# Weights of an involution made for two tile rows at once: 64 stationary columns instead of 32

## The chip, the cores and the metric

The kernel runs on one core of one Trainium2 chip. The time is the device time of one launch in microseconds (us). The runs are few and scatter by some tenths of a per cent, so medians are compared. Engines: PE is TensorE (its weight loads, PEld, overlap its matmuls), DVE is VectorE, ACT is ScalarE, POOL is GpSimd, SP is SyncE, which here only issues DMAs.

## The reference, cut to what matters

Two layers, each added to its input, on x of shape (32, 256, 32, 32) in float32: 32 images, 256 channels, 32 x 32 pixels.

```python
# layer 0: a 3x3 convolution 256 -> 256 in fp16, after a group norm
x = x + _L0_conv_ref(_gn(x), weight, bias)
# layer 1: an involution, after a group norm
x = x + _L1_conv_ref(_gn(x), w1, bn_gamma, bn_beta, bn_mean, bn_var, w2, b2)

def _L1_conv_ref(x, w1, bn_gamma, bn_beta, bn_mean, bn_var, w2, b2):
    y = einsum('oc,bchw->bohw', w1, x)              # 256 -> 64 features
    y = relu(y * scale + shift)                     # a batch norm with fixed numbers
    w = einsum('oc,bchw->bohw', w2, y) + b2         # 64 -> 16 groups x 49 taps
    # each pixel has its own 7x7 kernel for each of 16 groups of 16 channels
    out = einsum('bgkhw,bgckhw->bgchw', w.reshape(b, 16, 49, H, W), patches(x, 7, pad=3))
```

The change is in how `w` is made, 64 features to 784 numbers at every pixel, and how it is laid out for the last sum.

## The kernel before, in words

**Front.** `front(b)` is a generator that does one image up to the features: group norm on ScalarE, the 3x3 conv in fp16 on TensorE (L337, 72 matmuls of 128x128 with up to 512 columns, accumulated in `pc`), clamp and residual on VectorE (L351, L353), a second group norm into `xn`, the 1x1 conv to 64 features (`py`, L385), and their ReLU by ScalarE into `y_sb` (L392). `y_sb` has the 64 features on 64 partitions twice: rows 0 and 1 of every four image rows in the lower half of the partitions, rows 2 and 3 in the upper one. At last the pixels of `xn` are transposed (`pt`, L400) and copied into `pixels` (L404).

**Weights.** `weights(b, r0)` makes the taps of four image rows in one call, 8 calls an image. For each of two rows in a half and each of four pairs `t` of tap columns dj, the 32 pixels of a row are the stationary operand (64 features x 32 pixels), and two tap columns of `w2_sb` (2 x 112 numbers; the last pair has one, 112) are the moving rows. So 16 matmuls go to 8 tiles of the array, 2 row halves by 4 column quadrants of 32, into two PSUM tiles `pw0` and `pw1`. In the trace each fp32 matmul and its weight load leave two records each. `evict` (L439) adds the bias on VectorE and writes the taps to `w_sb`, ordered by the source row that a tap reaches (image row plus tap row minus 3), in a ring of 32 rows. Where a call's pieces cross the image's edge or the ring's end, `ring_pieces` splits them, into 4 to 8 evictions a call.

**Through DRAM.** `scatter(b, k, part)` (L480, 7 DMAs per k of 160 KB, issued by SP) writes the rows of tile row k (8 image rows, 4 tile rows an image) from `w_sb` to the DRAM tile `wd`, one tap column dj a DMA, shifted so that each source pixel has its window. `load_bands(b, k)` (L493, 14 DMAs on POOL's queue and 2 on SP's) reads them back as a band, with three bands in turn.

**Sums.** `sums(b, m)` (L518) multiplies the pixels (64 positions x 32 channels stationary, again 8 tiles of 64x32) by the band (up to 190 window pixels moving) into `acc`, and `add_windows` (L534, VectorE) adds a window to x. `store` writes x out.

**Order.** `manual_schedule` keeps the order of the program on every engine, and a loop over steps n writes it by hand. An image has 16 steps. In each step come first the fronts of some three images, one stage each, then `sums` (even steps, two per tile row), `add_windows` a step later, `weights` (even steps, 18 steps ahead of the same image's sums), scatters, the load of x, and the band loads (9 steps ahead of their sums, every fourth step). In steps relative to the first sums of an image:

| tile row k | scattered in steps | band loaded in step | its first sums in step |
|---|---|---|---|
| 0 | -13, -12 | -9 | 0 |
| 1 | -9, -8 | -5 | 4 |
| 2 | -5, -4 | -1 | 8 |
| 3 | -3, -2 | 3 | 12 |

Call c of `weights` (0 to 7) stands in step 2c - 18. On TensorE an even step thus runs: part of a front (conv, features or transposes), sums, weights; then an odd step's front, and so on.

Of the kernel before, what the change touches and what calls it, by code (L numbers as in the profile page):

```python
# [9 lines left out]
F32 = mybir.dt.float32  # L10
AF = mybir.ActivationFunctionType
ALU = mybir.AluOpType

P = 128
B, C, H, W = 32, 256, 32, 32
N = H * W
NT = 512
# [3 lines left out]
K1, PAD1 = 7, 3  # L21
TAPS = K1 * K1
CR = 64
G = 16
# [15 lines left out]
TR = RG * XR  # L40
SIDES = 2
JC = W // SIDES
K = H // TR
M = K * SIDES
WIN = XR + K1 - 1
# [6 lines left out]
V = 2  # L52
A = G // V
WB = G * WIN
PAD = V * (TR - XR)
WPIX = K1 * WB + PAD
SW = K1 * G
S = H + 2 * PAD1
T = 4
TW = P // T  # L60
PAIR = 3 * GC
PAIRS = G // 2
ROW = S * WPIX
WR = 4
NBAND = 3
SHARE = 8
NPIX = 6
RING = 32
SCRATCH = 4096
FRONT = -56  # L70
LOAD = -63
LEAD = 18
# [3 lines left out]
def tile_quant_conv_then_involution(  # L76
# [16 lines left out]
    nc = tc.nc  # L93
    PSUM = bass.MemoryType.PSUM

    const = ctx.enter_context(tc.tile_pool(name="const", bufs=1))
# [4 lines left out]
    ps_w = ctx.enter_context(tc.tile_pool(name="ps_w", bufs=1, space=PSUM))  # L101
# [39 lines left out]
    for t in sum(sum(sums_sb, []), []):  # L141
        nc.gpsimd.memset(t, 0.0)

    y_sb = [const.tile([P, N // 2], F32, name=f"y_{i}") for i in range(2)]
    bands = [const.tile([P, SIDES, WINC * WB + PAD], F32, name=f"band_{i}") for i in range(NBAND)]
    for t in bands[CH:]:
        nc.gpsimd.memset(t, 0.0)
# [2 lines left out]
        nc.gpsimd.memset(t, 0.0)  # L150


    w_sb = const.tile([P, 2, RING, A, WIN, V], F32, name="w_sb")
    wd = dram.tile([H, S, WPIX], F32, name="wd")
    acc = [ps_acc.tile([P, RG, NT], F32, name=f"acc_{d}") for d in range(SIDES)]

# [2 lines left out]
    for kh in range(CH):  # L159
        wf = bands[kh].rearrange("p d n -> p (d n)")[:, : K0 * K0 * C].rearrange("p (k c) -> p k c", c=C)  # L160
        nc.sync.dma_start(wf, w0[kh * P : (kh + 1) * P])
        staged.append(wf)
    w2_sb = const.tile([P, K1, SW], F32, name="w2_sb")
    for i in range(2):
        nc.sync.dma_start(w2_sb[i * CR : (i + 1) * CR], w2)
    b2_sb = const.tile([P, 2, 2, SW], F32, name="b2_sb")
    for dj in range(K1):
        t, e = divmod(dj, 2)
        for r in range(2):
            nc.sync.dma_start(b2_sb[t * TW : (t + 1) * TW, e, r], b2[dj].partition_broadcast(TW))  # L170

    bias_sb = const.tile([P, CH], F32, name="bias_sb")
    nc.sync.dma_start(bias_sb, bias0.rearrange("(h p) -> p h", p=P))
# [10 lines left out]
    bn_scale = const.tile([P, 1], F32, name="bn_scale")  # L184
    nc.vector.tensor_mul(bn_scale, bn[:, 0:1], bn_r)
    bn_shift = const.tile([P, 1], F32, name="bn_shift")
# [4 lines left out]
    for col, cols, at, n in (  # L191
# [4 lines left out]
        to = bass.AP(  # L196
            tensor=wd.tensor,
            offset=wd.offset + col * WPIX + at,
            ap=[[ROW, H], [WPIX, cols], [1, n]],
        )  # L200
# [88 lines left out]
    def front(b):  # L289
# [30 lines left out]
        for s in range(4 * len(units) + 2):  # L320
            u, i = divmod(s, 4)
            if u < len(units):
# [6 lines left out]
                for n in range(sum(CONV[:i]), sum(CONV[: i + 1])):  # L329


                    k = n if n < K0 * K0 else CH * K0 * K0 - 1 - n
                    kh, k = n // (K0 * K0), (k + K0 * K0 // 2) % (K0 * K0)
                    di, dj = k // K0 - PAD0, k % K0 - PAD0
                    r0, r1 = max(nt * RT, -di), min((nt + 1) * RT, H - di)
# [9 lines left out]
            u, i = divmod(s - 3, 4)  # L345
            if 0 <= u < len(units) and i < 3:
                nt, mh = units[u]
                cols = slice(nt * NT, (nt + 1) * NT)
                if i == 0:
                    q = work.tile([P, NT], F16, tag="q", name="q", bufs=1)  # L350
# [20 lines left out]
        for h in range(CH):  # L371
            yield
            to = xn[:, h].rearrange("p (k d r j) -> p d k r j", d=SIDES, r=TR, j=JC)
            at = xt[:, h].rearrange("p (k r d j) -> p d k r j", d=SIDES, r=TR, j=JC)
# [3 lines left out]
        py = ps_m.tile([P, NT], F32, tag="m", name="py")  # L378
        for r0 in range(0, H, WR):
            cols = slice(r0 // 2 * W, (r0 + WR) // 2 * W)  # L380
            for kh in range(CH):
                px = xn[:, kh].rearrange("p (k d r j) -> p k r d j", d=SIDES, r=TR, j=JC)[:, r0 // TR]
                for i in range(2):
                    r = r0 % TR + 2 * i
# [4 lines left out]
                        start=kh == 0,  # L389
                        stop=kh == CH - 1,  # L390
                    )
        nc.scalar.activation(y_sb[b % 2], py, AF.Relu, bias=bn_shift, scale=bn_scale)  # L392
        yield from stages(5)

        for m in range(0, M, 2):
# [7 lines left out]
            to = pixels[(b * M + m) // 2 % NPIX].rearrange("p i a (v c) -> p (i a) v c", c=GC)  # L403
            nc.scalar.copy(to[:, :, ::2], pt.rearrange("p i (a v c) -> p (i a) v c", v=2, c=GC))  # L404
            yield

    def weights(b, r0):

        pws = [ps_w.tile([P, 2, 2, SW], F32, tag=f"pw{i}", name=f"pw{i}") for i in range(2)]
        for r in range(2):  # L410
            for t in range(T):
                for i in range(2):
                    half = slice(i * CR, (i + 1) * CR)
                    dj = slice(2 * t, min(2 * t + 2, K1))
                    nc.tensor.matmul(  # L415
                        pws[i][t * TW : (t + 1) * TW, : dj.stop - dj.start, r],
                        y_sb[b % 2][half, (r0 // 2 + r) * W : (r0 // 2 + r + 1) * W],
                        w2_sb[half, dj],
                        start=True,
                        stop=True,  # L420
                    )
        for i in range(2):
            for e in range(2):
                p = P if e == 0 else (K1 // 2) * TW
                for r, rows, d0, d1, at in ring_pieces(b, r0 + 2 * i):
                    evict(pws[i][:p, e, r : r + rows], e, r, rows, d0, d1, at)

    def evict(of, e, r, rows, d0, d1, at):

        p = of.shape[0]  # L430
        to = w_sb[:p, e]
        to = bass.AP(
            tensor=to.tensor,
            offset=to.offset + at * WB + V * (K1 - 1 - d0),
            ap=[to.ap[0], [V * WIN, rows * A], [WB - V, d1 - d0], [1, V]],
        )
        of = of.rearrange("p r (a d v) -> p (r a) d v", a=A, v=V)
        bias = b2_sb[:p, e, r : r + rows].rearrange("p r (a d v) -> p (r a) d v", a=A, v=V)
        nc.vector.tensor_tensor(to, of[:, :, d0:d1], bias[:, :, d0:d1], ALU.add)  # L439

    def ring_pieces(b, r0):

        def place(r, d):
            s = r0 + r + d - PAD1
            return (b * H + s) % RING if 0 <= s < H else None

        def together(d):
            return place(0, d) is not None and place(1, d) == place(0, d) + 1  # L450

        pieces = []
        for rows, ok in (
            ((0, 2), together),
            ((0, 1), lambda d: place(0, d) is not None and not together(d)),
            ((1, 1), lambda d: place(1, d) is not None and not together(d)),
        ):
            d = 0
            while d < K1:
                d0 = d  # L460
                while d < K1 and ok(d) and place(rows[0], d) == place(rows[0], d0) + d - d0:
                    d += 1
                if d > d0:
                    pieces.append((*rows, d0, d, place(rows[0], d0)))
                else:
                    d += 1
        return pieces

    def scatter(b, k, part):

        at = (b * H + k * TR) % RING
        for dj in range(part, K1, 2):
            t, e = divmod(dj, 2)
            to = bass.AP(
                tensor=wd.tensor,
                offset=wd.offset + k * TR * ROW + dj * WPIX + (K1 - 1 - dj) * WB,
                ap=[[WPIX, TW], [ROW, TR], [1, WB]],
            )
            rows = w_sb[t * TW : (t + 1) * TW, e, at : at + TR]
            nc.sync.dma_start(to, rows.rearrange("p s a r v -> p s (a r v)"))  # L480

    def load_bands(b, k):

# [61 lines left out]
    def due(n, lag):  # L545

        b, i = divmod(n - lag, per)
        return (b, i) if 0 <= b < B else (None, None)

    with tc.manual_schedule():  # L550
        fronts = {}
        for n in range(FRONT, B * per + 2):
            b, i = due(n, FRONT)
            if i == 0:
                fronts[b] = front(b)
            later = list(fronts)
            for part in range(2):
                for b in list(later):
                    got = next(fronts[b], fronts)
                    if got is fronts:  # L560
                        fronts.pop(b)
                    if got is not LATER:
                        later.remove(b)
            if n == FRONT + CH:
                quantize_weights()
            b, i = due(n, 0)
            if b is not None and i % 2 == 0:
                sums(b, i // 2)
            b, i = due(n, 1)
            if b is not None and i % 2 == 0:  # L570
                add_windows(b, i // 2)
                if i // 2 == M - 1:
                    store(b, 1)
                    x_tiles.pop(b)

            b, i = due(n, 2)
            if b is not None and i == 2 * (M - 1 - SIDES):
                store(b, 0)
            b, i = due(n, -LEAD)
            if b is not None and i % 2 == 0:  # L580
                weights(b, i // 2 * WR)

            for part in range(2):
                b, i = due(n, -LEAD + 1 + part)
                if b is not None and i % 2 == 0:
                    for k in range(K):
                        if i // 2 == min((k + 1) * TR // WR, H // WR - 1):
                            scatter(b, k, part)
            b, i = due(n, LOAD)
            if i == 0 and b > 0:  # L590
                x_tiles[b] = load_x(b)

            b, i = due(n, 3 - 4 * NBAND)
            if b is not None and i % 4 == 0:
                load_bands(b, i // 4)
# [37 lines left out]
```

## Time and profile before

| | |
|---|---|
| median of three runs | 1375.84 us (1371.69 to 1378.53) |
| the profiled execution's own time | 1370.77 us |
| its span, first to last instruction | 1368.9 us |
| granted TensorE clock, mean | 0.988 |
| DMA | 369.93 MB, mean 270 GB/s; 280240 packets on SP's queue, 86016 on POOL's |
| weights, TensorE (L415) | 8192 records, 290.6 us busy |
| sums, TensorE (L518) | 16384 records, 428.5 us busy |
| conv, TensorE (L337) | 2304 records, 534.5 us busy |
| weights, VectorE (L439) | 1280 instructions, 331.4 us busy |
| band loads, POOL (L493) | 1792 DMAs, 978.0 us busy, 4.9 us from issue to landing |

How to read it: "busy" is the time in which at least one instruction of a group ran, so groups that overlap count the same time twice. A matmul's end is modelled and reaches past the point where its last column went in. "x32" counts instructions, and "64*32" is the tile of the array that an instruction uses (rows by columns). In a table of waits a line gives who waited for whom, then the time in total, how often, and the longest; "issue" is idle time without anything shown that holds the engine. In a table of stretches each engine has its busy time and number of instructions, then the granted clock, the DMA engines' busy share and GB/s. "Single records" are the trace's instructions one by one, with start and duration.

### The profile page before, as it was taken

What the parts mean: (1) busy time and instruction counts of PE and PEld (TensorE: products, weight loads), DVE (VectorE), ACT (ScalarE), POOL (GpSimd) and SP (SyncE); (2) the same over time, 40 slices, a digit from 0 to 9 for tenths busy, and PEclk for the clock granted to TensorE, in tenths of its full rate; (3) what the DMA queues carried; (4) which work ended last, traced back from release to release, by engine and by line L of the source; (5) the groups of instructions that cost most, each with busy time, mean ns of one, the idle gap of its engine ahead of it and who ended that gap; (6) DMA issues with size and microseconds to landing.
All of it is one profiled execution on the core that took longest, in us unless ns stands there. A gap on an engine that the chain in (4) does not pass through costs nothing.

```text
span 1368.9 us, 69378 instructions
## 1 busy us (share of the span) xinstructions
PE 1261.3 (92%) x29440; PEld 805.5 (59%) x29440; DVE 820.2 (60%) x2539; ACT 726.8 (53%) x1699; POOL 1012.1 (74%) x1818
## 2 busy tenths in 40 slices
PE   4799999999999999999999999999999999999664
PEld 2356666656665665666666566556656656666543
DVE  3366566666666666665666666656666666666542
ACT  4866565465655555665555565545555555553300
POOL 9057777778777777877777777777777777778875
PEclk9999999999999999999999999999999999999997
DMA  6089999999999999999999999999999999999995
GB/s 218 6 221 289 278 283 290 296 274 287 277 285 284 279 287 282 291 290 282 289 286 285 276 279 282 280 294 269 282 290 278 286 285 287 289 287 268 275 273 170
DMA packets 366563, 369.93 MB, mean 270 GB/s; under 512 B 78960, under 2 KB 308528, under 8 KB 366000
## 3 DMA queue, kind: packets, MB, share of 16 engines
q1 hardware_dynamic: 280240, 235.90, 58.0%
q0 software_dynamic: 86016, 129.60, 34.1%
q8 instruction: 234, 3.83, 1.2%
q14 instruction: 73, 0.60, 0.1%
HBM read 184.43 MB, written 180.76 MB: 267 GB/s over the span
## 4 chain that ended last, share of the span: by engine, by line
PE 72%; DMA 13%; issue 4%; POOL 3%; ACT 3%; SPq 2%; DVE 2%; POOLq 0%; DVEq 0%; ACTq 0%
PE pc L337 29%; PE acc L518 23%; PE pw L415 13%; DMA band<-wd 7%; PE py L385 4%; DMA wd<-w_sb 4%; PE pt L400 3%; POOL band L493 3%; ACT junk L224 1%; SPq L480 1%; DMA x<-in_x 1%; DMA out<-x 1%; DVE w_sb L439 1%; DMA w_sb<-in_w 1%; SPq L493 0%
## 5 line engine op out<-in xcount | busy, mean ns | idle before, releaser
L493 POOL DMA_DIRECT2D band<-wd x1792 | 978.0, 548 | 343.2 <-DMA band<-wd 209.9
L439 DVE TENSOR_TENSOR w_sb<-pw,b_sb 128x224 f32<-128x224 f32 (+7 forms) x1280 | 331.4, 324 | 434.7 <-PE pw L415 428.7
L337 PE MATMUL pc<-xq,wq 128*128 128x496 f16 (+3 forms) x2304 | 534.5, 378 | 30.6 <-ACT xq L283 24.3
L518 PE MATMUL acc<-band,pixels 64*32 64x190 f32 (+1 forms) x16384 | 428.5, 329 | 50.5 <-DMA band<-wd 28.0
L337 PEld LDWEIGHTS <-wq 128*128 128x128 f16 x2304 | 206.5, 98 | 324.3 <-issue 110.9
L518 PEld LDWEIGHTS acc<-band,pixels 64*32 64x32 f32 x16384 | 300.8, 106 | 141.8 <-issue 89.4
L415 PE MATMUL pw<-w_sb,y 64*32 64x224 f32 (+1 forms) x8192 | 290.6, 330 | 17.7 <-issue 16.8
L534 DVE TENSOR_TENSOR x<-acc,x 128x380 f32<-128x380 f32 (+1 forms) x512 | 262.3, 512 | 32.9 <-PE acc L518 24.0
L415 PEld LDWEIGHTS pw<-w_sb,y 64*32 64x32 f32 x8192 | 186.1, 105 | 48.3 <-issue 33.4
L404 ACT COPY pixels<-pt 128x512 f32<-128x512 f32 x128 | 73.7, 576 | 237.2 <-PE pt L400 237.2
L224 ACT ACTIVATE junk<-x 128x512 f16<-128x512 f32 (+1 forms) x192 | 146.4, 763 | 16.6 <-DVE bn_ve L182 6.0
L224 ACT ACTIVATE junk<-x,mean 128x1024 f16<-128x1024 f32 x128 | 147.1, 1149 | 4.3
L255 ACT ACTIVATE s<-back,eps 128x2 f32<-128x2 f32 x64 | 19.0, 296 | 198.6 <-DVE back L240 198.5
L351 DVE TENSOR_SCALAR q<-pc 128x512 f16<-128x512 f32 x128 | 87.1, 680 | 18.2 <-PE pc L337 18.1
L283 ACT ACTIVATE xn<-x,off,rstd 128x512 f32<-128x512 f32 x128 | 96.2, 800 | 0.0
L353 DVE SCALAR_TENSOR_TENSOR x<-q,bias_sb,x 128x512 f32<-128x512 f16 x128 | 94.6, 739 | 0.3
L400 PEld LDWEIGHTS pt<-ident,xn 128*128 128x128 f32 x512 | 63.3, 141 | 26.6 <-issue 2.7
L400 PE MATMUL pt<-ident,xn 128*128 128x128 f32 x512 | 77.3, 274 | 0.8 <-ACT pixels L404 0.7
L283 ACT ACTIVATE xq<-x,off,rstd 128x1024 f16<-128x1024 f32 x64 | 75.8, 1227 | 1.0 <-PE pc L337 0.9
L385 PEld LDWEIGHTS py<-xn,w_sb 128*64 128x64 f32 x2048 | 62.8, 138 | 16.8 <-issue 6.7
L385 PE MATMUL py<-xn,w_sb 128*64 128x64 f32 x2048 | 67.7, 224 | 2.8 <-ACT xn L283 2.2
L245 ACT ACTIVATE mean<-back 128x2 f32<-128x2 f32 x64 | 12.6, 196 | 101.2 <-DVE back L240 101.2
(40 smaller groups left out, 372.7 us busy)
## 6 DMA issues: line engine op xcount, KB each, us to landing
wd<-w_sb SPq DMA_DIRECT2D x896, 160.0 KB
band<-wd POOLq DMA_DIRECT2D x1792, 70.5 KB, 4.9
x<-in_x SPq DMA_DIRECT2D x64, 512.0 KB
out<-x SPq DMA_DIRECT2D x64, 512.0 KB
band<-wd SPq DMA_DIRECT2D x256, 70.5 KB
band<-in_w SPq DMA_DIRECT2D x2, 1152.0 KB
w_sb<-in_w SPq DMA_DIRECT2D x2, 196.0 KB
wd<-band SPq DMA_DIRECT2D x2, 180.0 KB
```

The source lines that it names most:

```text
L224: nc.scalar.activation(junk[:, n0:n1], src[:, h, n0:n1], func, bias=bias, accum_out=self.sums[:, i : i + 1])
L283: nc.scalar.activation(dst, src, AF.Identity, bias=self.off[:, one], scale=self.rstd[:, one])
L337: nc.tensor.matmul(pc.rearrange("p (r c) -> p r c", c=W)[:, r0 - nt * RT : r1 - nt * RT, c0:c1], wq[:, kh, k, mh * P : (mh + 1) * P], xq[: ...
L351: nc.vector.tensor_scalar(q, pc, F16_MAX, -F16_MAX, ALU.min, ALU.max)
L353: nc.vector.scalar_tensor_tensor(xt[:, mh, cols], q, bias_sb[:, mh : mh + 1], xt[:, mh, cols], ALU.add, ALU.add)
L385: nc.tensor.matmul(py[i * CR : (i + 1) * CR, cols], w1_sb[:, kh, :], px[:, r : r + 2], start=kh == 0, stop=kh == CH - 1,)
L400: nc.tensor.transpose(pt[:, i, h * P : (h + 1) * P], xn[:, h, (m + i) * P : (m + i + 1) * P], ident)
L415: nc.tensor.matmul(pws[i][t * TW : (t + 1) * TW, : dj.stop - dj.start, r], y_sb[b % 2][half, (r0 // 2 + r) * W : (r0 // 2 + r + 1) * W], w ...
L439: nc.vector.tensor_tensor(to, of[:, :, d0:d1], bias[:, :, d0:d1], ALU.add)
L493: queue.dma_start(band[j::JC, :, j * WB : j * WB + WPIX], src)
L518: nc.tensor.matmul(at[t * TW : (t + 1) * TW, h, :, f - top : l - top], px[p, a, v * GC : v * GC + TW], of[:, :, a, f - top : l - top, v], ...
L534: nc.vector.tensor_tensor(x_at, of, x_at, ALU.add)
```

## The change

`weights(b, n)` makes taps for two tile rows at once. Four calls serve tile rows 2a and 2a + 1 (a = 0, 1); an image still has 8 calls, in the same steps. For one row rho counted from the top of a tile row (-3 to 10, since rows above and below reach into it), the 32 pixels of that row in tile row 2a and the 32 pixels of the same row in tile row 2a + 1 together are the 64 stationary columns. `y_sb` is laid out so that these 64 lie side by side, with a row of zeros at either end for rows outside of the image. The moving rows are, for four tap columns dj (`QE`; the eighth is zero), the 1 to 7 tap rows d that land inside of the tile row: 64 numbers for each tap row, 64 to 448. Two column quadrants `t` of 64 take tap columns 0 to 3 and 4 to 6. `UNITS` deals the 14 rows rho out to the four calls, two lists for the two halves of the partitions. A call has 8, 8, 8 or 4 matmuls with 512, 448, 448 or 384 columns per tile of the array.

`w_sb` becomes two blocks of two tile rows (a = 0, 1), each 8 source rows by 4 tap columns, of the same size in all; no taps are left out at the image's edge, and no ring is left. Each row rho has one eviction, 14 per a. A scatter still moves 32 partitions x 8 rows x 160 numbers, now from rows that lie four tap columns apart. The scatters of both tile rows of a block wait for its fourth call. In the steps of the table above they are now: k = 0 in -11, -10; k = 1 in -9, -8; k = 2 in -3, -2; k = 3 in -1, 0. The band loads stay in their steps. At the start, `b2_sb` is loaded with 2 DMAs instead of 14, after a memset; `y_sb` (two) and one column block of `w2_sb` get memsets too.

```diff
+BLK = TR
+QB = H // BLK
 T = 4
 TW = P // T
+QT = 2
+QE = 4
+QW = P // QT
-RING = 32
+UNITS = (((4, -3), (3, 10)), ((0, 8), (7, -1)), ((1, 9), (6, -2)), ((5,), (2,)))
...
-    y_sb = [const.tile([P, N // 2], F32, name=f"y_{i}") for i in range(2)]
+    y_sb = [const.tile([P, N // 2 + 2 * W], F32, name=f"y_{i}") for i in range(2)]
+    for t in y_sb:
+        nc.gpsimd.memset(t, 0.0)
...
-    w_sb = const.tile([P, 2, RING, A, WIN, V], F32, name="w_sb")
+    w_sb = const.tile([P, 2, BLK, QE, WB], F32, name="w_sb")
...
-    w2_sb = const.tile([P, K1, SW], F32, name="w2_sb")
+    w2_sb = const.tile([P, QT * QE, SW], F32, name="w2_sb")
+    nc.gpsimd.memset(w2_sb[:, K1:], 0.0)
...
-    b2_sb = const.tile([P, 2, 2, SW], F32, name="b2_sb")
-    for dj in range(K1):
-        t, e = divmod(dj, 2)
-        for r in range(2):
-            nc.sync.dma_start(b2_sb[t * TW : (t + 1) * TW, e, r], b2[dj].partition_broadcast(TW))
+    b2_sb = const.tile([P, QE, SW], F32, name="b2_sb")
+    nc.gpsimd.memset(b2_sb, 0.0)
+    for t in range(QT):
+        dj = slice(t * QE, min((t + 1) * QE, K1))
+        nc.sync.dma_start(b2_sb[t * QW : (t + 1) * QW, : dj.stop - dj.start], b2[dj].partition_broadcast(QW))
...
-        nc.scalar.activation(y_sb[b % 2], py, AF.Relu, bias=bn_shift, scale=bn_scale)
+        to = y_sb[b % 2][:, W:-W].rearrange("p (r k c) -> p k r c", k=QB, c=W)
+        of = py.rearrange("p (k r c) -> p k r c", k=QB, c=W)
+        nc.scalar.activation(to, of, AF.Relu, bias=bn_shift, scale=bn_scale)
...
-    def weights(b, r0):
...
-    def evict(of, e, r, rows, d0, d1, at):
...
-    def ring_pieces(b, r0):
...
+    def weights(b, n):
+
+        a, n = divmod(n, len(UNITS))
+        pws = [ps_w.tile([P, NT], F32, tag=f"pw{i}", name=f"pw{i}") for i in range(2)]
+        ats = [0, 0]
+        for rhos in zip(*UNITS[n]):
+            for i, rho in enumerate(rhos):
+                d0, d1 = max(0, PAD1 - rho), min(K1, BLK + PAD1 - rho)
+                d = d1 - d0
+                of = pws[i][:, ats[i] : ats[i] + QE * d * G]
+                k, r = divmod(rho, BLK)
+                half = slice(i * CR, (i + 1) * CR)
+                y0 = (((r // 4) * 2 + r % 2) * QB + 2 * a + k) * W + W
+                for t in range(QT):
                     nc.tensor.matmul(
+                        of[t * QW : (t + 1) * QW].rearrange("p (q n) -> p q n", n=d * V),
+                        y_sb[b % 2][half, y0 : y0 + QW],
+                        w2_sb[half, t * QE : (t + 1) * QE].rearrange("p e (a n) -> p (e a) n", a=A)[:, :, V * d0 : V * d1],
                         start=True,
                         stop=True,
                     )
+                ats[i] += QE * d * G
+        ats = [0, 0]
+        for rhos in zip(*UNITS[n]):
+            for i, rho in enumerate(rhos):
...
+                to = bass.AP(
+                    tensor=to.tensor,
+                    offset=to.offset + (rho + d0 - PAD1) * QE * WB + V * (K1 - 1 - d0),
+                    ap=[to.ap[0], [V * WIN, QE * A], [QE * WB - V, d], [1, V]],
+                )
...
+                nc.vector.tensor_tensor(to, of, bias, ALU.add)
+                ats[i] += QE * d * G
...
     def scatter(b, k, part):
 
-        at = (b * H + k * TR) % RING
+        a, k2 = divmod(k, 2)
         for dj in range(part, K1, 2):
-            t, e = divmod(dj, 2)
+            t, e = divmod(dj, QE)
...
-            rows = w_sb[t * TW : (t + 1) * TW, e, at : at + TR]
-            nc.sync.dma_start(to, rows.rearrange("p s a r v -> p s (a r v)"))
+            p = t * QW + k2 * TW
+            nc.sync.dma_start(to, w_sb[p : p + TW, a, :, e])
...
             if b is not None and i % 2 == 0:
-                weights(b, i // 2 * WR)
+                weights(b, i // 2)
 
             for part in range(2):
-                b, i = due(n, -LEAD + 1 + part)
-                if b is not None and i % 2 == 0:
-                    for k in range(K):
-                        if i // 2 == min((k + 1) * TR // WR, H // WR - 1):
-                            scatter(b, k, part)
+                for k in range(K):
+                    b, i = due(n, -LEAD + 1 + part + k % 2 * 2)
+                    if b is not None and i == 8 * (k // 2) + 6:
+                        scatter(b, k, part)
```

More of the change, by code (lines that the diff above doesn't have):

```diff
@@ L162, in tile_quant_conv_then_involution @@
         staged.append(wf)
-    w2_sb = const.tile([P, K1, SW], F32, name="w2_sb")
+    w2_sb = const.tile([P, QT * QE, SW], F32, name="w2_sb")
+    nc.gpsimd.memset(w2_sb[:, K1:], 0.0)
     for i in range(2):
-        nc.sync.dma_start(w2_sb[i * CR : (i + 1) * CR], w2)
-    b2_sb = const.tile([P, 2, 2, SW], F32, name="b2_sb")
-    for dj in range(K1):
-        t, e = divmod(dj, 2)
-        for r in range(2):
-            nc.sync.dma_start(b2_sb[t * TW : (t + 1) * TW, e, r], b2[dj].partition_broadcast(TW))
+        nc.sync.dma_start(w2_sb[i * CR : (i + 1) * CR, :K1], w2)
+    b2_sb = const.tile([P, QE, SW], F32, name="b2_sb")
[3 more added lines that the diff above has]
+        nc.sync.dma_start(b2_sb[t * QW : (t + 1) * QW, : dj.stop - dj.start], b2[dj].partition_broadcast(QW))
     bias_sb = const.tile([P, CH], F32, name="bias_sb")
@@ L405, in front @@
             yield
-    def weights(b, r0):
[L409 to L414, printed above, removed]
+    def weights(b, n):
[11 more added lines that the diff above has]
+                for t in range(QT):
                     nc.tensor.matmul(
-                        pws[i][t * TW : (t + 1) * TW, : dj.stop - dj.start, r],
-                        y_sb[b % 2][half, (r0 // 2 + r) * W : (r0 // 2 + r + 1) * W],
-                        w2_sb[half, dj],
+                        of[t * QW : (t + 1) * QW].rearrange("p (q n) -> p q n", n=d * V),
+                        y_sb[b % 2][half, y0 : y0 + QW],
+                        w2_sb[half, t * QE : (t + 1) * QE].rearrange("p e (a n) -> p (e a) n", a=A)[:, :, V * d0 : V * d1],
                         start=True,
@@ L421, in weights @@
                     )
[L422 to L426, printed above, removed]
-    def evict(of, e, r, rows, d0, d1, at):
[L430 to L439, printed above, removed]
@@ L441, in ring_pieces @@
-    def ring_pieces(b, r0):
[L445 to L467, printed above, removed]
+                ats[i] += QE * d * G
@@ new lines, in weights @@
+        ats = [0, 0]
+        for rhos in zip(*UNITS[n]):
+            for i, rho in enumerate(rhos):
+                d0, d1 = max(0, PAD1 - rho), min(K1, BLK + PAD1 - rho)
+                d = d1 - d0
+                of = pws[i][:, ats[i] : ats[i] + QE * d * G]
+                to = w_sb[:, a]
+                to = bass.AP(
[3 more added lines that the diff above has]
+                )
+                of = of.rearrange("p (q d v) -> p q d v", d=d, v=V)
+                bias = b2_sb.rearrange("p e (a d v) -> p (e a) d v", a=A, v=V)[:, :, d0:d1]
+                nc.vector.tensor_tensor(to, of, bias, ALU.add)
+                ats[i] += QE * d * G
```

## The prediction, as put on record before the changed kernel ran

> **What bounds the kernel now.** First the page's summary by engine and its strip of 40 slices.
>
> ```profile
> PE 1261.3 (92%) x29440; PEld 805.5 (59%) x29440; DVE 820.2 (60%) x2539; ACT 726.8 (53%) x1699; POOL 1012.1 (74%) x1818
> ...
> PE   4799999999999999999999999999999999999664
> ...
> DMA  6089999999999999999999999999999999999995
> ```
>
> TensorE (PE) is full from the third slice to the 37th, and the 16 DMA engines from the fourth. A ramp stands ahead of this stretch and a tail behind it. So I read the stretch from 100 to 1270 us alone: its busy times, then what TensorE waited for in it.
>
> ```profile
> 100.00:1270.00 1170.00, 1131.05 (x26764) 724.37 (x26751) 737.83 (x2294) 648.38 (x1519) 887.62 (x1627) 1.00 0.98 284
> ```
> ```profile
> PE acc L518 <- issue: 14.6, 22, 1.8
> PE pw L415 <- issue: 14.1, 22, 1.6
> PE pc L337 <- issue: 4.7, 6, 1.7
> PE acc L518 <- DMA band<-wd: 3.8, 6, 1.4
> ```
>
> TensorE is busy 1131 of 1170 us. Of its 39 us of idle time, 33.4 (14.6 + 14.1 + 4.7) are "issue", time in which nothing shown holds it, and 3.8 are waits for a band's DMA. DMA is 0.98 busy at 284 GB/s but hardly ever late. So a nanosecond more on TensorE is paid in full, while a nanosecond less soon meets DMA. An image takes some 40.4 us here (first 1x1-conv rows `py` at 203.05, 241.32, 282.80, 323.78), 2.5 us per step n.
>
> **TensorE, streaming.** In the single records of the trace, the starts of one array tile's records with 224 columns lie 188 ns apart (0.84 ns a column), and each fp32 matmul makes two records. Before, a weights call gives each of 8 tiles two matmuls of 224 columns (the last column quadrant only 112): 4 x 188 = 752 ns. After, four calls give each of 4 tiles 512, 448, 448 and 384 columns, 1792 in all, and four calls before gave 4 x 448 = 1792. So the longest tile streams as long as before, and streaming changes by nothing. There are fewer tiles, each with longer rows, and that is a wash.
>
> **TensorE, the change of array shape.** Now the rows around two weights calls, one from the first image, when no sums run yet, and one from the middle (start, time, line, shape).
>
> ```profile
> 67.17 0.60 PE L400 MATMUL pt<-ident,xn 128*128 128x128 f32 x4
> 67.70 0.97 PE L415 MATMUL pw<-w_sb,y 64*32 64x224 f32 x32
> 68.61 2.08 PE L337 MATMUL pc<-xq,wq 128*128 128x496 f16 x9
> ```
> ```profile
> 706.19 1.60 PE L518 MATMUL acc<-band,pixels 64*32 64x190 f32 x64
> 707.56 0.98 PE L415 MATMUL pw<-w_sb,y 64*32 64x224 f32 x32
> 708.48 2.08 PE L337 MATMUL pc<-xq,wq 128*128 128x512 f16 x9
> ```
>
> In the first, tile shape goes from 128*128 to 64*32: the weights begin 0.07 us before the recorded end of the transposes (67.17 + 0.60 = 67.77), and the conv starts 0.84 us after that end. In the second, sums and weights share shape 64*32: the weights begin 0.23 us before the recorded end of the sums (707.79), quadrant by quadrant as each comes free, and the conv starts 0.69 us after it. In the single records of the nine calls ahead of the first sums, all behind a shape change, this is 0.837 us seven times and 0.852 once (the conv of the ninth waited for `xq`); over 144 calls behind sums its median is 0.688. The same work costs 0.149 us more behind a change of shape. After the edit weights are 64*64, so every call behind sums pays such a change: the ends are 0 (64*32 and 64*64 count as one shape) and 0.30 us (twice the price, since none of the rows is 64*64). I take 0.149, the row of the same instruction. The conv and `py` (128*128 to 128*64, 722.59 + 2.08 against 724.60) also show the 0.07, so a change of columns alone counts.
>
> The page "TensorEngine Tiling (Array Packing)" of the Trainium skill, section Key Properties, says that changing the tiling mode, not just the tile, drains the engine, and it lists 64x32 and 64x64 as two modes; no row here has that pair. By it the lower end 0 is excluded, and the sum below would start from 0.149.
>
> Of 256 calls 9 are already behind a change and some 10 run in the tail, where TensorE idles: 237 x 0.149 = **+35.3 us**.
>
> The same page's section Instruction Overhead puts some 60 cycles on each matmul. A call has on average 3.5 records per tile instead of 4, so that rule gives an estimate of -3 us for all calls, with a cycle taken as one column of the conv's rows (217 ns for 512 columns, 0.42 ns). The trace's 188 ns for 224 columns are two such cycles a column and leave no room for a fixed part, and the sum goes by the trace.
>
> **TensorE, fewer instructions.** 128 weights matmuls an image become 56. Records fall by 4608 matmuls and as many weight loads, 9216 of 58880, 16%. If the 33.4 us of "issue" idle go with their number, -5; if all that stands before weights goes and half of that before sums, 14.1 + 7.3 = -21; at least 0. I take **-8**, nearer to the proportional row.
>
> **VectorE.** Two rows by shape price the eviction.
>
> ```profile
> L439 DVE TENSOR_TENSOR w_sb<-pw,b_sb 128x224 f32<-128x224 f32 x384 | 147.4, 384 | 289.7 <-PE pw L415 287.8 <-DMA wd<-w_sb 1.6
> ...
> L439 DVE TENSOR_TENSOR w_sb<-pw,b_sb 128x16 f32<-128x16 f32 x128 | 20.8, 162 | 0.0
> ```
>
> (384 - 162) / 208 = 1.067 ns a column, 145 ns fixed. After: 28 evictions an image with 7168 columns, 28 x 145 + 7168 x 1.067 = 11.7 us, 375 in all against 331.4: +43 us, 0.17 a call. VectorE is 63% busy in the stretch, and with calls 4.7 us apart the next one finds its PSUM free. Cover is incomplete where sums wait for the adds queued behind evictions (their weight loads, L518, waited 16.2 us in 36 waits for L534 in the stretch). Ends 0 and 237 x 0.17 = 40; I take **+2**.
>
> **Scatters and bands.** Scatters of k = 0 and 2 move two steps (5 us) later; k = 1 stays, k = 3 moves two steps too; the band loads stay where they are. In the single records the last scatter of k = 0, 1, 2, 3 is issued 6.9, 8.0, 8.2, 11.3 us before the first load of its band (medians), and the last load 9.6 to 10.3 us before its sums, while a load lands in 4.9 us. After, 1.9, 8.0, 3.2 and 6.3 us are left. On SP, four scatters of the next tile row stand between the scatters of k = 0 and 2 and their loads' two DMAs, 3.6 us of issue, so SP barely blocks; POOL blocks until the scatter lands. If scatters land as loads do, bands 0 and 2 start 3.0 and 1.7 us later, within the 4.8 us (9.7 - 4.9) of slack. Descriptors, bytes and the ring's size stay. I take **0**; ends 0 and 31 us (one us per image).
>
> **Start and end.** Two DMAs for b2 replace 14.
>
> ```profile
> 3.85 12.62 SPq L170 DMA_DIRECT2D b_sb<-in_b  x14
> ```
>
> But they now wait for a memset that POOL reaches behind those of `pixels` (until 14.2 us) and four new ones, estimated at 1.5 to 2.6 us from the 768-column ones (1.14 us). Done at 15.7 to 16.8, plus 2 x 0.9 of issue: 17.5 to 18.6 against 16.5. SP is in order, so the next image's x (24.53), and the conv that waited 5.76 us for it at 40.63, come 1 to 2 later: **+1.5** (ends 0 and 3). In the tail (1300 to 1369) PE is busy 38 of 69 us and the chain is band loads; the last image's k = 2 scatter is two steps later, partly within its 8.2 us: **+3** (ends 0 and 6). ScalarE's y copy keeps its 512 columns (0.77 us, 32 times): 0.
>
> **Sum.** Against the profiled execution's 1370.8 us (span 1368.9): 1370.8 + 35.3 - 8 + 2 + 0 + 1.5 + 3 = 1404.6. That run lies 5 us under the median of the three, 1375.84, so I forecast **1407**, halfway: +2.3% on the median. Some 0.5% is what a measurement can tell from no change.
>
> **Rivals.**
> - A, faster: 64*32 and 64*64 overlap like two calls of one shape, and "issue" falls by 21. 1370.8 - 21 + 2 + 1.5 + 3 = 1356. It decides once a shape change costs under (21 - 6.5) / 237 = 0.06 us. For it: the row count on both shapes is 64. Against: conv to `py` changes only columns and has the gap. 0.10.
> - B, absorbed: DMA at 0.98 sets the pace, and TensorE's 35 us fill its 39 idle ones: 1370.8 + 4.5 = 1375. Against: only 3.8 us of that idle time is a wait for DMA. 0.10.
> - C, bands late: POOL's waits on landings outlast the slack, 1 us per image on top: 1405 + 31 = 1436. For it: POOL is 76% busy in the stretch and DMA full. Against: 4.8 us of slack. 0.10.
> - D, the change doesn't do what it says: four 64*64 tiles don't stream at once, 0.75 us more per call: 1405 + 180 = 1585. Against: `py`'s two 128*64 tiles start 6 ns apart. 0.02.
>
> The forecast has 0.68. Faster 0.10 (A), same 0.10 (B), slower 0.80 (forecast, C, D). The range 1370 to 1440 leaves out A and D, 0.12, and a part of the forecast's outer ends (price 0.30 with VectorE uncovered).
>
> **What the new profile would show.** Weights in 64*64 rows of up to 448 columns, 3584 records; beginning 0.07 us, not 0.23, before the recorded end of the sums; conv about 0.84 after that end on average over the four kinds of call. TensorE's "issue" waits lower, evictions near 375 us and 896, DMA share near 0.95, waits for bands still a few us. I am wrong if weights still overlap the sums' end, or if waits for `band` reach tens of us.

## The result, and the profile after

The changed kernel takes 1440.89 us (median of four runs, 1437.47 to 1443.81) against 1377.18 for the kernel before in the same job: 1.043 times as long, 95% interval 1.039 to 1.047. The forecast was 1407, so the sign was right and the loss was twice what I had put. The median lies 0.9 us past the upper end of the range; 1.043 times the 1375.84 from which I had started is 1435. The profiled execution has a span of 1439.0 us, 70.1 more than before.

First the page's summary by engine and its slices.

```profile
PE 1303.9 (91%) x24832; PEld 755.6 (53%) x24832; DVE 809.0 (56%) x2155; ACT 733.7 (51%) x1699; POOL 1017.2 (71%) x1822
...
PE   4899899999999999999899999999999998998764
...
DMA  6089999999999999999999999999999999998886
```

TensorE has lost 4608 matmuls and looks about as full as before (91% against 92%). The stretch from 100 to 1270 us and TensorE's waits in it say more.

```profile
100.00:1270.00 1170.00, 1109.43 (x21399) 644.28 (x21401) 691.87 (x1853) 632.82 (x1466) 845.72 (x1545) 0.98 0.96 269
```
```profile
PE acc L505 <- DMA band<-wd: 42.4, 25, 4.4
PE acc L505 <- DMA wd<-w_sb: 14.3, 7, 3.4
...
PE pw L431 <- issue: 1.0, 1, 1.0
PE acc L505 <- issue: 0.9, 3, 0.5
```

The 33.4 us of "issue" idle have shrunk to 1.9, and in their place TensorE waits 56.7 us (42.4 + 14.3) for bands or what they hang on, where it had waited 3.8. This is what the prediction had named as the sign of being wrong, waits for `band` of tens of us. DMA moves 269 GB/s instead of 284, and the granted clock is 0.98 instead of 1.00. The clock is not the loss: the conv's matmuls take 379 ns on average, against 378 before. In the single records 61 us of such gaps stand ahead of the first sums of tile row k = 2, in 30 of the images. Here is one of them.

```profile
696.51 0.60 PE L410 MATMUL pt<-ident,xn 128*128 128x128 f32 x4
697.04 1.57 PE L505 MATMUL acc<-band,pixels 64*32 64x190 f32 x64
698.54 1.10 PE L431 MATMUL pw<-w_sb,y 64*64 64x448 f32 x16
699.57 2.08 PE L345 MATMUL pc<-xq,wq 128*128 128x496 f16 x9
701.48 0.60 PE L410 MATMUL pt<-ident,xn 128*128 128x128 f32 x4
706.08 2.79 PE L505 MATMUL acc<-band,pixels 64*32 64x190 f32 x64 [3.99 <-DMA band<-wd]
```

The same rows show the change of shape. The weights begin 0.07 us before the recorded end of the sums (697.04 + 1.57 = 698.61 against 698.54), where before it was 0.23. From that end to the conv the four kinds of call take 0.959, 0.856, 0.876 and 0.738 us (medians of 58 each), 0.857 on average against 0.688: +0.169 us a call, 237 calls, +40 us of TensorE. The forecast had +35.

How that band came late is told by the rows of SP and POOL.

```profile
677.81 6.62 SPq L467 DMA_DIRECT2D wd<-w_sb  x7
684.54 0.92 SPq L526 DMA_DIRECT2D out<-x  x1
685.77 4.36 SPq L467 DMA_DIRECT2D wd<-w_sb  x4
690.29 1.22 SPq L480 DMA_DIRECT2D band<-wd  x2
```
```profile
689.58 4.93 POOL L480 DMA_DIRECT2D band<-wd  x9 [3.29 <-PE acc L505]
694.96 2.87 POOL L480 DMA_DIRECT2D band<-wd  x5 [0.46 <-DMA band<-wd]
```

The seven scatters of k = 2 are issued until 684.43, and POOL stands idle until 689.58; of all that these loads need, the landing of those scatters is the only thing that comes so late. (The releaser named is what came last by the profile; the sums that had used this band's place, the last of the image before, began at 677.79 and take 1.6 us, so they are not it.) It is so in most images: in 26 of the 28 in the middle POOL stops ahead of the loads of k = 2, and starts 4.4 to 6.2 us after the last scatter is issued, when the place has been free for 7.5 us or more. In the kernel before it stops there in 6 of 28. From there the 14 loads take until 697.83 to issue, and the sums start at 706.08.

**Where the 70.1 us are.** By the `py` rows: the ramp up to the second image's is 1.5 us shorter, 30 images take 40.03 -> 42.10 us each (+62.0), and the tail from the start of the last `py` grows from 84.1 to 93.6 (+9.6). So the question is what sets the pace of an image. POOL's waits before, in the same stretch, are these.

```profile
POOL band L493 <- DMA band<-wd: 197.5, 251, 3.0
POOL band L493 <- issue: 51.0, 79, 2.4
POOL band L493 <- DMA wd<-w_sb: 18.6, 25, 1.9
```

With its 887.6 us of issuing they make 1154.7 of 1170 us. POOL was not 76% busy with slack to spare. It went from one band's loads to the next, held up mostly by waits for loads of bands (197.5). By the single records, an image has four bands of 7.67 us of issue and 2.13 of waits inside, and 1.03 us ahead of its bands in all: 40.2, against a period of 40.34. In the changed kernel it is 4 x (7.70 + 1.94) + 3.78 = 42.3 against 42.40, and of the 3.78 us, 2.04 stand ahead of k = 2 and 1.01 ahead of k = 3 (before: 0.17 and 0.34). What the waits inside a band hang on, 8.5 us of an image before, no run isolates.

The table of POOL's waits in the changed kernel doesn't show this by name.

```profile
POOL band L480 <- DMA band<-wd: 180.9, 213, 3.8
POOL band L480 <- issue: 57.1, 62, 4.7
POOL band L480 <- DMA wd<-w_sb: 23.2, 24, 3.8
POOL band L480 <- DMA x<-in_x: 21.3, 20, 3.9
POOL band L480 <- PE pt L410: 16.0, 9, 2.7
POOL band L480 <- PE acc L505: 15.3, 8, 3.5
```

Waits put down to scatters are only 4.6 us more than before (23.2 against 18.6), while 52.6 us have come up under x, `pt` and `acc`, of which only x had any (1.4). The row of 689.58 is such a case: by the times it is a wait for scatters, and it stands under `acc`. That scatters are behind the other stops too rests on the single records above, and on e2 and e4 below.

### The profile page after: what moved, and what is told of

Its sections match the earlier page's. It is cut to its first block, busy times and chain, and to the rows that moved or that the text cites. A ratio compares the mean times of both kernels' runs of the same rounds, so it can differ in the third digit from the quotient of the medians.

```text
span 1439.0 us, 59553 instructions
## 1 busy us (share of the span) xinstructions
PE 1303.9 (91%) x24832; PEld 755.6 (53%) x24832; DVE 809.0 (56%) x2155; ACT 733.7 (51%) x1699; POOL 1017.2 (71%) x1822
## 4 chain that ended last, share of the span: by engine, by line
DMA 40%; PE 35%; POOL 9%; SPq 8%; issue 4%; DVE 2%; ACT 2%; POOLq 0%
DMA band<-wd 22%; PE pc L345 13%; DMA wd<-w_sb 13%; PE acc L505 12%; POOL band L480 9%; PE pw L431 7%; SPq L467 6%; DMA x<-in_x 5%; PE py L393 2%; SPq L480 2%; DVE w_sb L453 1%; DMA band<-in_w 1%; PE pt L410 1%; ACT junk L232 1%; ACT xq L291 0%
## 5 line engine op out<-in xcount | busy, mean ns | idle before, releaser
L453 DVE TENSOR_TENSOR w_sb<-pw,b_sb 128x448 f32<-128x448 f32 (+6 forms) x896 | 320.8, 418 | 533.8 <-PE pw L431 528.0
L505 PEld LDWEIGHTS acc<-band,pixels 64*32 64x32 f32 x16384 | 307.1, 108 | 191.3 <-issue 134.7
L431 PE MATMUL pw<-w_sb,y 64*64 64x448 f32 (+6 forms) x3584 | 265.0, 404 | 1.0 <-issue 1.0
L431 PEld LDWEIGHTS pw<-w_sb,y 64*64 64x64 f32 x3584 | 115.3, 136 | 140.7 <-issue 109.1
```

The costliest lines, as they stand in the source:

```text
L431: nc.tensor.matmul(of[t * QW : (t + 1) * QW].rearrange("p (q n) -> p q n", n=d * V), y_sb[b % 2][half, y0 : y0 + QW], w2_sb[half, t * QE : ...
L453: nc.vector.tensor_tensor(to, of, bias, ALU.add)
L505: nc.tensor.matmul(at[t * TW : (t + 1) * TW, h, :, f - top : l - top], px[p, a, v * GC : v * GC + TW], of[:, :, a, f - top : l - top, v], ...
```

## The experiments

The theory after the result: the price of the shape change and the late band add up. The rival: the late band is all, and TensorE's 40 us only fill its idle time. The kernel before took 1384 to 1387 us in these jobs; each ratio is to it in the same job.

**Tiles of 64*32 again, in the changed kernel** (e1), **weights and scatters two steps earlier** (e2), **and both** (e3). In e2 the scatters of k = 0, 2 and 3 are back in the steps that they had in the kernel before; those of k = 1 are two steps ahead of theirs.

```diff
+                    for c in range(0, QW, TW):
                         nc.tensor.matmul(
-                            of[t * QW : (t + 1) * QW]...
-                            y_sb[b % 2][half, y0 : y0 + QW],
+                            of[t * QW + c : t * QW + c + TW]...
+                            y_sb[b % 2][half, y0 + c : y0 + c + TW],
```
```diff
-LEAD = 18
+LEAD = 20
```

> The changed kernel with each 64-column matmul split into two of 32 columns, so that weights use the array shape 64*32 of the sums again (7168 records instead of 3584, same columns per tile, same evictions, same steps). Theory (price of the shape change, plus the k = 2 band that comes late): the 0.857 us from the recorded end of the sums to the conv fall to about 0.69, TensorE gets some 40 us back, the band waits stay or grow by up to 20: 1405 to 1425 us. Rival (the late band alone sets the pace, TensorE's extra time only fills its waits): 1435 to 1445. Rival (the 64*64 form itself is slow, not the change of shape): no way to tell here, also near 1405.

> The changed kernel with weights and scatters two steps (5 us) earlier (LEAD 20 instead of 18); band loads stay. Theory: the k = 2 scatters are back in the steps of before, so the 61 us of waits ahead of the sums of k = 2 go almost wholly, and what stays is the price of the shape change less the issue idle time that went: 1380 to 1395 us. Rival (bands are late because DMA as a whole is full or because SP is blocked behind its own band loads, not because of the scatters' steps): 1430 to 1445.

> The changed kernel with both edits: 64*32 tiles and weights two steps earlier. Theory: both prices are gone and part of the lower issue idle time stays: 1345 to 1375 us, at or below the kernel before (1377). Rival (issue idle time follows the number of instructions, 7168 weights records against 8192 before, and bands stay late): 1390 or more.

Measured: e1 1451.28 us (1.045, 1.039 to 1.051), e2 1385.37 (0.997, 0.993 to 1.001), e3 1392.09 (1.005, 1.002 to 1.007). In e1 the sums' end to the conv fell to 0.699 us on average, so the price is one of the shape change and TensorE had its time back; it gained nothing. In e2 the price of 0.857 stands on every call and the kernel is as fast as before. Of the three only e2 came where my theory had put it: a price of the shape change would have shown as a gain in e1 and in e3 against e2, and it didn't. The rival held: as far as these runs can tell, the loss goes with the steps alone.

```profile
100.00:1270.00 1170.00, 1140.57 (x22220) 662.94 (x22214) 719.87 (x1922) 647.37 (x1514) 875.84 (x1605) 1.00 0.97 279
```

This is the stretch in e2. TensorE is busy 1140.57 of 1170 us, more than in the kernel before (1131.05): the added time went where "issue" idle time had been.

**The kernel before with nothing but the later steps** (e4).

```diff
-                b, i = due(n, -LEAD + 1 + part)
-                if b is not None and i % 2 == 0:
-                    for k in range(K):
-                        if i // 2 == min((k + 1) * TR // WR, H // WR - 1):
-                            scatter(b, k, part)
+                for k in range(K):
+                    b, i = due(n, -LEAD + 1 + part + k % 2 * 2)
+                    if b is not None and i == 8 * (k // 2) + 6:
+                        scatter(b, k, part)
```

> The kernel before with nothing changed but the steps of its scatters, which get those of the changed kernel (k = 0 and 2 and 3 two steps later). Theory: the k = 2 band comes late as in the changed kernel, 40 to 60 us of waits ahead of its sums, part of it in place of issue idle time: 1410 to 1430 us. Rival (what I forecast: slack covers it): 1375 to 1385.

Measured: 1443.36 us (1.038, 1.032 to 1.044), with 8192 weights records on 64*32 and no other change. Its waits in the stretch:

```profile
PE acc L518 <- DMA band<-wd: 61.5, 30, 4.9
PE pw L415 <- issue: 9.7, 10, 2.0
PE acc L518 <- issue: 5.4, 6, 1.2
```

The later steps alone make the loss, within the intervals (1.038 against 1.043): 56.8 us on this job's 1386.59, although "issue" idle time fell to 16.2 us (9.7 + 5.4 + 1.1 on the conv). I had expected 1410 to 1430 us, so the loss is larger than the theory made it.

**SP's part.** In the changed kernel SP stands at its own two band loads until the scatter has landed, in order, with the next scatters behind. Its waits in the stretch, before and after:

```profile
SPq L493 <- DMA wd<-w_sb: 23.0, 38, 1.6
```
```profile
SPq L480 <- DMA wd<-w_sb: 228.0, 147, 6.3
```

So I put all 16 loads of a band on POOL, in the changed kernel (e5) and in the one before (e6), and later 3 on SP instead of 2 (e9 to e12).

```diff
-SHARE = 8
+SHARE = 99
```
```diff
-SHARE = 8
+SHARE = 5
```

> The changed kernel with all 16 loads of a band on POOL's queue (2 of them were on SP's). Theory: SP, in order, stands at its two band loads until the scatter just issued has landed (245.7 us of such waits in the changed kernel, 24 before), and the next scatters stand behind them; with the loads off SP these waits are gone, the scatters go out as soon as their evictions are done, and the band of k = 2 is late by less: 1395 to 1415 us. Rival: the band is late because POOL itself must wait for a scatter two steps later, whatever SP does; two more DMAs on POOL make that worse: 1440 to 1455.

> The control for that: the kernel before with all 16 loads of a band on POOL. Its SP waits 24 us for scatters at its band loads, so nothing to gain there; POOL issues 256 DMAs more (0.55 us each, 141 us, POOL is 76% busy). Both theories: 1380 to 1400 us, no more than 15 above the kernel before.

Measured: e5 1537.24 us (1.108, 1.100 to 1.114), e6 1526.22 (1.098, 1.089 to 1.106). My expectations for both were far off, and e6 is the best witness for POOL: 256 DMAs more at 0.55 us are 141 us, and 1526.22 - 1384.47 is 141.8. Every issue added to that queue is paid in full.

```profile
L493 POOL DMA_DIRECT2D band<-wd x2048 | 1117.3, 548 | 360.8 <-DMA band<-wd 230.6 <-DMA wd<-w_sb 56.7 <-issue 53.6
```

**Is TensorE or the DMA engines' bandwidth the pace?** Half of the conv left out (e7), and a seventh of the scatters left out (e8), both in the kernel before.

```diff
                 for n in range(sum(CONV[:i]), sum(CONV[: i + 1])):
+                    if n >= K0 * K0:
+                        continue
...
-                        stop=n == CH * K0 * K0 - 1,
+                        stop=n == K0 * K0 - 1,
```
```diff
         for dj in range(part, K1, 2):
+            if b > 0 and dj == K1 - 1:
+                continue
```

> The kernel before without the conv's second half of input channels (9 of 18 matmuls per conv tile are left out, so the conv is only half computed): TensorE loses some 15.6 us of 40.4 an image (9 x 8 x 0.217). Theory (DMA sets the pace in the steady stretch, TensorE only just keeps up): the time hardly falls, 1350 to 1385 us. Rival (TensorE sets the pace, as I forecast; then DMA at 0.98 busy is only a neighbour that would let the time fall by its 2% and no more): 1340 to 1350. The two are near each other; the DMA share and the band waits tell more, 0.98 to 1.0 with tens to hundreds of us of band waits in both, so the time itself is the floor that DMA gives.

> The kernel before without the scatters of the seventh tap column (dj = 6) after the first image, so the later images use stale weights there: 20 of 370 MB less DMA (5.4%), 4 of 28 scatters an image less for SP, nothing less on TensorE. Theory (DMA sets the pace): the steady stretch falls until TensorE's own time holds it, 1131 of 1170 us, so 1335 to 1360 us. Rival (TensorE sets the pace): 1370 to 1390, no difference.

Measured: e7 1384.51 us against 1384.47 (1.000, 0.996 to 1.004); e8 1375.40 (0.992, 0.989 to 0.996). The stretch in e7:

```profile
100.00:1270.00 1170.00, 965.02 (x25496) 661.27 (x25501) 728.46 (x2268) 649.85 (x1516) 879.77 (x1613) 0.95 0.98 281
```

TensorE is 166 us less busy (1131.05 - 965.02), at a granted clock of 0.95 instead of 1.00, and the time is the same to 0.4%. TensorE is not the pace. With 5.4% less to move in e8, DMA's share falls to 0.94 and the time by 0.8%, while POOL's sum stays at 4 x (7.67 + 2.16) + 1.0 = 40.3 of a period of 40.49. Bandwidth alone is not the pace either: e7 came where I had put it for DMA as the pace, and e8 where I had put it for TensorE.

**One load less on POOL's queue** (e9 to e12: the kernel before, the changed one, e2 and e3, each with SHARE 5).

> The kernel before with 3 of a band's 16 loads on SP's queue instead of 2, so 13 on POOL's instead of 14 (128 fewer in all, 0.55 us each). Theory (POOL's queue, which issues band loads one behind the other all the time, sets the pace of an image): POOL's part of an image falls from 40.3 to some 37.5 us, TensorE's own 39 us takes over, 1335 to 1355 us against some 1384 on this chip. Rival (DMA bandwidth or TensorE sets the pace): 1375 to 1390.

> The changed kernel with the same edit. Theory: POOL has 2.2 us an image less to issue and still waits for the late scatters of k = 2 and 3 (2.75 us more an image than before): 42.4 - 2.2 = 40.2 an image, 1375 to 1400 us. Rival (the late scatters are paid by TensorE itself, whatever POOL has to issue): 1430 to 1445.

> The changed kernel with weights and scatters two steps earlier and 13 loads on POOL. Theory: POOL is no longer the pace, TensorE is, with the price of the shape change (0.169 us a call) in the open: 10 to 40 us above the next kernel, 1355 to 1380 us. Rival (the shape change stays hidden behind something else, DMA bandwidth for one): within 5 us of the next kernel.

> The same with weights on 64*32 tiles, so without the change of shape. Theory: TensorE at its lowest and POOL out of the way, 1330 to 1355 us, the fastest of all. Rival: the same as the kernel ahead of it.

Measured: e9 1431.35 us (1.034, 1.029 to 1.039), e10 1510.78 (1.091, 1.086 to 1.097), e11 1385.04 (0.999, 0.996 to 1.002), e12 1400.46 (1.009, 1.006 to 1.013). None came out as I expected. POOL's waits in e9 tell why:

```profile
POOL band L493 <- DMA band<-wd: 184.7, 226, 3.4
POOL band L493 <- DMA wd<-w_sb: 127.1, 61, 6.5
```

The third load on SP makes the scatters later, and POOL waits 127.1 us for them instead of 18.6. POOL had less to issue and stood still instead: 4 x (7.12 + 1.95) + 6.05 = 42.3 of a period of 42.52. So SP has no room to give either. What the whole change costs in such pairs grows with the loads on SP: 11 us with none (e5 less e6), 64 with two, 79 with three (e10 less e9). That fits SP's waits at its own loads as a carrier of the lateness. It isn't proof: in e5 and e6 an image takes 45 us, so the steps are 12% longer, and no run took SP's waits away at an unchanged pace.

In e11 POOL's waits for scatters, 74.9 us, cost nothing, as the images take what they take in e2 (40.77 and 40.80 us). DMA is 1.00 busy there. A second ceiling, close above the first, is the likeliest reason that freeing POOL brought nothing, but no run isolates it. That e3 and e12 are slower than e2 and e11, with less work on TensorE, stays open.

## Why the prediction was right and where it failed

The sign came out right by luck. Of the 33.8 us that my sum added, the 29.3 of TensorE and VectorE (35.3 - 8 + 2) don't show in the time, and the 62 us of the 30 images come from the term that I had put at 0. Rival C's 1436 is near to the measured time in the same way: it adds 31 us for late bands to the 29.3 that don't show.

- **"A nanosecond more on TensorE is paid in full."** This failed. None of the terms that I drew from it is in the result. The change of shape was sized well, 0.169 us a call (forecast 0.149; +40 us against +35.3); the idle "issue" time went from 33.4 to 1.9 us, where I had -8. e2 has both and is level with the kernel before; e7 takes 166 us from TensorE and changes nothing. I read "busy 97%, waits small" as the pace. But the small waits showed only that bands came just in time, from a queue that ran without a pause. This is rival B's mechanism (something else sets the pace), with a queue in the place of DMA's bandwidth.
- **"Scatters and bands: 0."** This is the step that made the loss, rival C, and its price was 1 us an image in my text against 2.06 measured. My estimate of how much later the loads start was right for k = 2 (1.7 us; its stop grew by 1.87), too high for k = 0 (3.0 against some 0.1), and k = 3, which I had at none, grew by 0.67; POOL's stops grew by 2.75 us an image in all. The error came after it: I set them against 4.8 us of slack before a band's sums. First, I had misread that slack. In the single records before, the last load of a band on POOL is issued 7.1 to 7.4 us ahead of its first sums (medians), not 9.6 to 10.3; with 4.9 us to land, some 2.4 are left, and in some images none. In these two rows of the kernel before, the sixth load of the first, issued at 709.26, is the last of its band. The sums of the second still had to wait for that band, 6.75 us later.

```profile
706.40 3.94 POOL L493 DMA_DIRECT2D band<-wd  x7 [0.81 <-DMA band<-wd]
```
```profile
716.01 1.60 PE L518 MATMUL acc<-band,pixels 64*32 64x190 f32 x64 [0.29 <-DMA band<-wd]
```

  Second, such slack helps once. POOL's sum leaves it no time in which to catch up, so a stop moves the bands behind it too; in the changed kernel the first sums of k = 2 wait 3.7 us already in the second image. "SP barely blocks" failed as well: its waits at its own loads went from 23.0 to 228.0 us.
- **VectorE +2.** I had set a sum of durations (375 us) against a busy time (331.4). The sum of durations came out as forecast (896 x 418 ns, 375 us), but before it was 1280 x 324 ns, 415 us. On the other measure, evictions fell from 331.4 to 320.8 us busy. No loss shows.
- **Start +1.5.** It was 1.5 us less: SP's `bias`, `w1` and `bn` loads were put ahead of the two b2 DMAs, and the next x was issued at 20.55 instead of 24.53.
- **End +3.** It was +9.6. It goes with the steps: the same tail is 100.0 us in e4 and 86.1 in e2, against 84.1 before.
- **Streaming 0, rival D.** Right: four 64*64 tiles stream together. In the call at 698.54 they start 7 ns apart, and the call takes 1.10 us for 512 columns a tile, where one after the other at 0.84 ns a column and two records each they would take 3.4.
- C's price, 1 us an image, was a round number. POOL's own sum of issue and waits was not worked out, and it would have shown a queue without room.

## What to carry to other kernels

Before an engine is taken as the pace, add up each in-order queue: its issuing plus its waits on its own earlier work. Here a queue whose sum filled the stretch was the pace at 76% busy, and what delayed its head was paid image by image. A change that batches work (two tile rows for one) moves the hand-over of the first half; what that does to the queue behind it can outweigh all that is gained on the engine. Whoever takes work off one queue should ask first if the queue that gets it waits in order for the very thing it delays.

## What the runs showed of the hardware

- Going from 64*32 to 64*64 tiles, with the same 64 rows, costs what a change between any other two shapes cost here: the next matmul starts some 90 to 100 ns after the last column has gone in (an estimate from single records, by 0.42 ns a column in fp16 and 0.84 in fp32), where calls of one shape overlap. Per call that is 0.158 us (0.857 in the changed kernel, 0.699 in e1).
- Among kernels of about one time, TensorE's "issue" idle time in the stretch is less with fewer instructions, but not in proportion: 33.4 us with 8192 weights records (before), 28.6 with 7168 (e3), 2.6 with 3584 (e2). Where waits for bands are long it is less too: 16.2 with 8192 (e4). What it is stays open.
- DMA moved 284 GB/s at a busy share of 0.98 before and 269 at 0.96 after, so less for the same share; no run shows why.
